# Two-layer transformer kernel: layer 1's scores in two stretches, divisions queued ahead of rotary sums, and inputs transposed by VectorE in 32x32 squares that change places by way of memory

## The chip, the cores and the metric

The kernel runs on one core of a Trainium2 chip, as one program. The metric is the time of an execution on the device in microseconds (us); lower is better. Before the change the median of three runs is 939.76 us (939.63 to 940.93). The profile is of one further execution. Engines are named as in the profile: PE is TensorE (PEld its weight loads), DVE VectorE, ACT ScalarE, POOL GpSimd, SP the engine that issues most DMAs.

## What is computed

Input x is 8 batches of 512 tokens by 256 channels, float32. Two layers follow each other; each normalises its input and adds an attention part and a feed-forward part to x.

```python
# layer 1 (names L0_*)
xn = layernorm(x)
q, k, v = xn @ Wq + bq, xn @ Wk + bk, xn @ Wv + bv      # 16 heads of 64
q, k = rope(q), rope(k)
attn = softmax(causal(q @ k.T / 8))                     # per head, 512 x 512
attention = (attn @ v) @ Wo + bo
x_scale = max(abs(xn)) / 127                            # over all batches
ffn = int8(xn / x_scale) @ int8_weight.T * x_scale * weight_scale + bias
x = x + attention + ffn
# layer 2 (names L1_*): a gated comparison of all tokens with all, and a
# feed-forward part of three 256 x 256 products
```

The change lies in layer 1's attention, whose steps fill most of the program, and in how layer 1 keeps its transposed normalised input.

## The kernel before

**Steps.** Layer 1 works in 16 steps, numbered `at`; a step is half of the heads (8) of one batch, so `b, g = divmod(at, 2)` gives batch and half. The order of instructions on every engine is written by hand: the loop `for at in range(1, last)` (L813) calls one helper after another, each appends its instructions to the queues of the engines that it uses, and every engine takes its queue strictly in order. Step 0 stands before the loop, the last step and layer 2 behind it.

**Projections.** `project_qk` (L387) makes q or k for four heads: TensorE multiplies the transposed input `xnT` with weights into PSUM (`pq`, L400), ScalarE copies it out with the bias (`l`, L405), and SP copies `l` to `y` with groups of 32 partitions swapped (L407). `turn_qk` (L410) is the rotary embedding: VectorE multiplies `l` with cosines into `h` and `y` with sines in place (both L417), and GpSimd adds the two (the rotary sum, L432). `project(at, which)` calls `project_qk` twice. `project_v` (L434) makes v (`pv`, L443), ScalarE copies it (L449), and it goes through memory to lie in another order (`va`, `vr`; `load_v`, L455).

**Scores.** The 512 queries of a head are 16 strips of 32; strip i needs 32(i+1) keys. Two strips fill one PSUM bank per half of the heads, eight heads lie beside each other, and `RUNS` (L34) cuts the strips into five runs: (15; 14, 0), (13, 1; 12, 2), (11, 3; 10, 4), (9, 5; 8, 6) and (7). For a run, `scores` (L469) lets TensorE multiply in tiles of 64x32 (`sc`, L480); `soften` (L487) lets VectorE add the mask and take each row's maximum (`nm`, L508) and ScalarE the exponential and its sum (L512); `divide` (L518) takes the reciprocals on VectorE (L523) and multiplies the rows with them on GpSimd (L531), or with `on_act` on ScalarE (L529) for the run's second pair of strips; `turn` (L539) transposes them in 32x32 squares on VectorE (L551). `weigh` (L560) multiplies all of a step's rows with v (`av`, L568), `keep_weighed` (L576) copies the result out on ScalarE, and `output_product` (L356) and `add_output` (L368) multiply with Wo (`pw`, L362) and add on VectorE (L371).

**Order of a step.** scores run 0 of this step; weigh of the step before; scores run 1; q projection of the next step; scores run 2; v projection of the next step; in even steps the transposes of the next batch's input; scores runs 3 and 4; output product of the step before; k projection of the step after next. Each run is softened, divided and turned close behind its scores.

**PSUM.** All results of TensorE go to tiles of one pool with 8 buffers, one for each of the eight banks of 512 float32 a partition (`bank`, L60). A tile takes over a bank that an earlier tile has left; its first matmul waits until the readers of that earlier tile are done.

**Input.** `look_at` (L291) takes a batch's statistics on VectorE, `prepare` (L305) normalises it (L171) and takes its greatest magnitude (L301). `transpose_x` (L312) transposes it on TensorE (8 transposes of 128x128, `pxt`, L318), ScalarE copies the two results into `xnT` (L321), and `keep_input` (L309) stores it in memory (`xnf`). Later, `fetch_input` (L183) brings it back, `round_input` (L187) scales and rounds it on GpSimd, and `clip` (L192) limits it on VectorE for the int8 product (`add_quantised`, L199). Batches 0 and 1 are fetched and clipped in steps 12 and 13, the others in the tail and layer 2.

Of the kernel before, what the change touches and what calls it, by code (L numbers as in the profile page):

```python
# [8 lines left out]
F32 = mybir.dt.float32  # L9
# [7 lines left out]
P = 128  # L17
# [27 lines left out]
def two_layers(  # L45
# [25 lines left out]
        return xpool.tile([P, NT, D], F32, tag="x1", name=name, bufs=3)  # L71

    x1_far = [far.tile([P, NT * D], F32, name=f"x1f_{b}") for b in range(B - 1)]
    xn_far = [far.tile([P, NK * S], F32, name=f"xnf_{b}") for b in range(B)]

    def load_x(b, parts=1):
        t = xpool.tile([P, NT, D], F32, tag="x", name=f"x_{b}")
# [103 lines left out]
        nc.sync.dma_start(dst.rearrange("p t n -> p (t n)"), x1_far[b])  # L181

    def fetch_input(b, r):  # L183
        nc.sync.dma_start(r.rearrange("p a n -> p (a n)"), xn_far[b])
        return r

    def round_input(r):  # L187

        r = r.rearrange("p a n -> p (a n)")
        nc.gpsimd.tensor_scalar(r, r, xs[:, 1:2], ROUND, ALU.mult, ALU.add)  # L190

    def clip(r, xq):  # L192

        r = r.rearrange("p a n -> p (a n)")
        xq_ = xq.rearrange("p k n -> p (k n)")
        nc.vector.tensor_scalar(xq_, r, -ROUND, -128.0, ALU.add, ALU.max)
        nc.vector.tensor_scalar(xq_, xq_, 127.0, 127.0, ALU.min, ALU.min)

    def add_quantised(b, half, xq, u):  # L199
        rows = slice(2 * half, 2 * half + 2)  # L200
        acc = bank(f"acc_{b}_{half}").rearrange("p (j n) -> p j n", j=2)
        for j in range(2):
            tok = bass.ts(2 * half + j, P)
            for k in range(NK):
                nc.tensor.matmul(  # L205
                    acc[:, j, :], xq[:, k, tok], w8b[:, k, :], start=(k == 0), stop=(k == NK - 1)
                )
        u = u.rearrange("p (j n) -> p j n", j=2)
        for j in range(2):
            nc.vector.scalar_tensor_tensor(  # L210
                u[:, j, :], acc[:, j, :], xs[:, 0:1], rw[:, 0, :], ALU.mult, ALU.mult
            )
        nc.gpsimd.tensor_tensor(x1s[b][:, rows, :], x1s[b][:, rows, :], u, ALU.add)
# [41 lines left out]
    with ExitStack() as c0:  # L255
# [49 lines left out]
        def prepare(b):  # L305
            norm_input(b)
            greatest_of(b)

        def keep_input(b):  # L309
            nc.sync.dma_start(xn_far[b], xnT[b].rearrange("p k n -> p (k n)"))  # L310

        def transpose_x(b):  # L312
            xn = normed.pop(b)
            xnT[b] = whole(f"xnT_{b}")
            for k in range(NK):
                pb = bank(f"pxt_{b}_{k}")
                for t in range(NT):
                    nc.tensor.transpose(  # L318
                        pb[:, bass.ts(t, P)], xn[:, t, bass.ts(k, P)], ident
                    )  # L320
                nc.scalar.copy(xnT[b][:, k, :], pb)  # L321
            if b > 0:
                keep_input(b)

# [62 lines left out]
        def project_qk(at, which):  # L387


            b, g = divmod(at, NG)  # L390
            w = wqkv[which]

            l, y = (
                prob.tile([P, 2, S], F32, tag="p", name=f"{tag}_{at}_{which}") if at == 1 else
                work.tile([P, 2, S], F32, tag=tag, name=f"{tag}_{at}_{which}", bufs=2) for tag in "ly"
            )
            for t in range(2):
                pb = bank(f"pq_{at}_{which}_{t}")
                for k in range(NK):
                    nc.tensor.matmul(  # L400
                        pb, w[:, g, k, bass.ts(t, P)], xnT[b][:, k, :],
                        start=(k == 0), stop=(k == NK - 1),
                    )
                bias = BIAS + which * NP + 2 * g + t
                nc.scalar.activation(l[:, t, :], pb, AF.Identity, bias=cs[:, bias : bias + 1])  # L405
            for n in range(4):
                nc.sync.dma_start(y[bass.ts(n ^ 1, Q)], l[bass.ts(n, Q)])  # L407
            evicted[at, which] = l, y
# [25 lines left out]
        def project_v(at, halves=(0, 1)):  # L434
# [3 lines left out]
            for half in halves:  # L438
                v = work.tile([P, 4, 2, P], F32, tag="v", name=f"v_{at}_{half}", bufs=2)
                for j in range(2):  # L440
                    pb = bank(f"pv_{at}_{half}_{j}")
                    for k in range(NK):
                        nc.tensor.matmul(  # L443
                            pb.rearrange("p (g n) -> p g n", g=2),
                            xnT[b][:, k, bass.ts(2 * half + j, P)],
                            wqkv[2][:, 2 * g : 2 * g + 2, k, :],
                            start=(k == 0), stop=(k == NK - 1),
                        )
# [87 lines left out]
        def pitch(c):  # L536
            return NT * 4 - 4 * c - 1

        def turn(at, run):  # L539

            if at not in turned:
                turned[at] = [
                    prob.tile([P, 2, 4 * pitch(c) + 1, Q], F32, tag=f"t{c}", name=f"t_{at}_{c}", bufs=1)
                    for c in range(NT)
                ]
            for i in (i for us in RUNS[run] for i in us):
                p = chances.pop((at, i))
                for c in range(i // 4 + 1):
                    n = min(4, i + 1 - 4 * c)
# [10 lines left out]
        def weigh(at):  # L560
            t = turned.pop(at)
            banks = [bank(f"av_{at}_{j}") for j in range(4)]
            for i in by_turns:
                c, m = divmod(i, 4)
                for j in range(4):
                    rows = slice(j * Q, j * Q + Q)
                    for e in range(2):
                        nc.tensor.matmul(  # L568
                            banks[j][e * L : e * L + L, i * Q :],
                            vs[at][rows, m, c, bass.ts(e, L)],  # L570
                            t[c][rows, e, m * pitch(c) + m : m * pitch(c) + NT * 4 - 4 * c, :],
                            start=(i == by_turns[0]), stop=(i == by_turns[-1]),
                        )
# [25 lines left out]
        def fetch_late(b):  # L599
# [1 line left out]
                tag, k = {2: ("vr", 0), 3: ("vr", 1), 4: ("t1", 0), 5: ("t1", 1), 6: ("t2", 0)}[b]  # L601
                fetch_output(b, by_tokens(cuts[tag][k]))
            if b > 2:
                late[b] = fetch_input(b, cuts["wo"][b % 2].rearrange("p (k n) -> p k n", k=NK))

        def round_late(b):
            round_input(late[b])

        def clip_late(b):
            xq = work.tile([P, NK, S], BF16, tag="xq", name=f"xq_{b}")  # L610
            clip(late.pop(b), xq)
            return xq

# [196 lines left out]
        x_next.append(load_x(2))  # L810
        turn(0, 3)
        project(2, 1)
        for at in range(1, last):  # L813
            b, g = divmod(at, NH)
            two = at + 2 <= last
            if g == 0 and b < B - 1:
                fetch(b)
            scores(at, 0)
            turn(at - 1, 4)
            soften(at, 0)  # L820
            if at == last - 3:
                scale_of_x()
            weigh(at - 1)
            keep_weighed(at - 1)
            if at == 1:
                load_rest()
                load_second()
                fetch(0)
            turn_qk(2 * at + 2, 1)
            load_v(at)  # L830
            if at in (last - 3, last - 2):
                s_ = at - last + 3
                fetch_output(s_, output_tile(f"x1e_{s_}"))
                xnl = fetch_input(s_, work.tile([P, NK, S], F32, tag="xnl", name=f"xnl_{s_}"))
            divide(at, 0)
            turn_qk(2 * at + 3, 1)
            if at == last - 2:
                first_norm = norm(0, xpool.tile([P, NT, D], F32, tag="x", name="yn_0"))
            scores(at, 1)
            soften(at, 1)  # L840
            turn(at, 0)
            if at == 2:
                look_at(2)
            elif at == 4:
                spread_rest()
                spread_second()
            elif g == 1 and 1 <= b < B - 2:
                look_at(b + 2)
            divide(at, 1)
            if at == last - 1:  # L850
                first_norm()
            project(at + 1, 0)
            if at in (last - 3, last - 2):
                round_input(xnl)
            scores(at, 2)
            soften(at, 2)
            turn_qk(2 * at + 2, 0)
            turn(at, 1)
            if at in (last - 3, last - 2):
                xq = work.tile([P, NK, S], BF16, tag="xq", name=f"xq_{s_}")  # L860
                clip(xnl, xq)
            divide(at, 2)
            if at == 2:
                prepare(2)
            elif g == 1 and 1 <= b < B - 2:
                prepare(b + 2)
            if at == last - 1:
                turn_qk(2 * at + 3, 0)
            if at == 1:
                nc.gpsimd.tensor_tensor(bob, bob, rw[:, 2, :], ALU.add)  # L870
                add_biases(0)
            project_v(at + 1)
            if at == last - 1:
                break
            if g == 0 and b < B - 1:
                transpose_x(b + 1)
                if b + 2 < B:
                    x_next.append(load_x(b + 2))
            scores(at, 3)
            soften(at, 3)  # L880
            turn_qk(2 * at + 3, 0)
            turn(at, 2)
            divide(at, 3)
            scores(at, 4)
            soften(at, 4)
            if at in (last - 3, last - 2):
                for half in range(2):
                    add_quantised(s_, half, xq, line(f"u_{s_}_{half}"))
            finish(at - 1)
            turn(at, 3)  # L890
            if two:
                project(at + 2, 1)
            divide(at, 4)
            if g == 0 and b < B - 1:
                add_biases(b)
            if at == last - 4:
                greatest()


        at = last  # L900
        scores(at - 1, 3)
        soften(at - 1, 3)
        nc.sync.dma_start(w2, second.rearrange("j (k p) n -> p j k n", p=P))
        turn(at - 1, 2)
        divide(at - 1, 3)
        scores(at - 1, 4)
# [21 lines left out]
        divide(at, 1)  # L928
        keep_weighed(at - 1)
        load_v(at)  # L930
        late[2] = fetch_input(2, work.tile([P, NK, S], F32, tag="xnl", name="xnl_2"))
        add_biases(B - 1)
        turn(at, 0)
        scores(at, 2)
# [143 lines left out]
```

## Time and profile before

| what | value |
|---|---|
| time, median of 3 runs | 939.76 us (939.63 to 940.93) |
| the profiled execution: its time | 939.1 us |
| the profiled execution: its span, first to last instruction | 937.2 us |
| granted TensorE clock, mean | 0.999 of full |
| 600 to 700 us: busy PE, DVE, ACT, POOL | 98.79, 91.29, 59.59, 74.45 us |
| 700 to 937.2 us: the same | 233.49, 182.11, 118.84, 89.96 us |
| rows of L417, y and h: mean | 1729 ns, 1243 ns, 64 each |
| row of L432: mean | 2596 ns, 62 |
| row of L551 (all shapes): mean | 366 ns, 640 |

A row of the profile has the line of the kernel, the engine, the operation, output<-inputs by tile names, partitions x elements, and a count; times are busy time and the mean of one. A timeline has the start and length of each instruction, or of several alike that follow each other; an idle time ahead of it stands in brackets with what ended it. The chain follows the last instruction back, step by step, to what released it. The span is the time between first and last instruction; the execution's own time is somewhat longer.

### The profile page before, as it was taken

To read this page: it belongs to the slowest core of one execution; us is meant where nothing else is said; L and a number is where in the kernel's file an instruction comes from. 1 tells how busy PE (TensorE), PEld (TensorE's weight loads), DVE (VectorE), ACT (ScalarE), POOL (GpSimd) and SP (SyncE) were. 2 spreads that over 40 slices of the span, in tenths; PEclk is the share of its full clock that TensorE was granted. 3 is DMA by queue.
4 is the path that set the end of the run, shared out by engine and by line. 5 is a ranking of instruction groups with operands and counts; after the bars stand their busy time and mean duration, and the time that the engine had idled before them with its cause. 6 is when DMAs were issued, how large, how long until landed. Compare 5 with 4: busy or idle time off the path is not lost.

```text
span 937.2 us, 27414 instructions
## 1 busy us (share of the span) xinstructions
PE 923.8 (99%) x10491; PEld 600.8 (64%) x10491; DVE 787.4 (84%) x2431; ACT 533.0 (57%) x1488; POOL 540.0 (58%) x688
## 2 busy tenths in 40 slices
PE   9998999999999999999999999999999999999998
PEld 5446565656666575757565656666657777777776
DVE  4998889898799889978997899899899588888854
ACT  3585555656575656474747566555667434445553
POOL 2676765655665757566665756678666424444311
PEclk9999999999999999999999999999999999999999
DMA  7667453525443545263535435453444132211011
GB/s 212 193 166 201 112 128 126 122 80 138 146 105 96 133 136 131 75 159 92 136 91 160 108 98 137 136 145 106 103 114 126 47 101 79 76 57 39 23 34 34
DMA packets 60930, 105.40 MB, mean 112 GB/s; under 512 B 7552, under 2 KB 38272, under 8 KB 60800
## 3 DMA queue, kind: packets, MB, share of 16 engines
q1 hardware_dynamic: 58928, 102.01, 40.1%
q10 hardware_dynamic: 1872, 1.64, 0.7%
q8 instruction: 83, 1.36, 0.6%
q14 instruction: 47, 0.39, 0.1%
HBM read 39.14 MB, written 28.84 MB: 73 GB/s over the span
## 4 chain that ended last, share of the span: by engine, by line
PE 92%; DVE 4%; issue 1%; ACT 1%; POOL 1%; SPq 0%; DMA 0%; DVEq 0%; ACTq 0%; POOLq 0%
PE pq L400 22%; PE av L568 14%; PE sc L480 13%; PE pw L362 12%; PE pv L443 10%; PE po L727 5%; PE pg L689 3%; PE pvv L701 3%; PE pk L674 3%; PE trc L714 1%; PE plr L240 1%; PE c L646 1%; DVE t L551 1%; PE acc L205 1%; DVE p L508 1%
## 5 line engine op out<-in xcount | busy, mean ns | idle before, releaser
L512 ACT ACTIVATE p<-p,nm 128x64 f32<-128x64 f32 (+15 forms) x512 | 259.9, 512 | 123.1 <-DVE nm L508 98.3
L531 POOL TENSOR_SCALAR p<-p,rs 128x512 f32<-128x512 f32 (+4 forms) x504 | 263.3, 543 | 44.0 <-DVE rs L523 41.9
L432 POOL TENSOR_TENSOR h<-h,y 128x1024 f32<-128x1024 f32 x62 | 161.0, 2596 | 188.9 <-DVE y L417 106.6
L508 DVE CUSTOM_DVE_ANT_0 p<-sc,cmask 128x64 f32<-128x64 f32 (+15 forms) x512 | 190.3, 434 | 61.5 <-PE sc L480 61.5
L551 DVE STREAM_TRANSPOSE t<-p 128x256 f32<-128x256 f32 (+3 forms) x640 | 192.1, 366 | 18.2 <-POOL p L531 18.1
L480 PE MATMUL sc<-h,h 64*32 64x416 f32 (+15 forms) x4096 | 138.7, 393 | 1.9 <-POOL h L432 1.2
L568 PE MATMUL av<-t,vr 32*64 32x192 f32 (+15 forms) x4096 | 128.8, 392 | 4.0 <-issue 4.0
L568 PEld LDWEIGHTS av<-t,vr 32*64 32x64 f32 x4096 | 123.2, 131 | 9.1 <-issue 7.8
L480 PEld LDWEIGHTS sc<-h,h 64*32 64x32 f32 x4096 | 78.8, 106 | 76.0 <-issue 56.5
L405 ACT ACTIVATE l<-pq,cs 128x512 f32<-128x512 f32 x128 | 84.7, 683 | 66.8 <-PE pq L400 54.4
L417 DVE TENSOR_TENSOR y<-y,cs 128x1024 f32<-128x1024 f32 x64 | 110.7, 1729 | 5.8 <-DMA y<-l 5.3
L362 PE MATMUL pw<-wo,att 128*128 128x256 f32 x512 | 114.8, 382 | 0.0
L400 PE MATMUL pq<-xnT,wq 128*128 128x512 f32 x256 | 114.6, 599 | 0.2 <-ACT xnT L321 0.2
L443 PE MATMUL pv<-wv,xnT 128*128 128x512 f32 x256 | 114.3, 599 | 0.0
L400 PE MATMUL pq<-xnT,wk 128*128 128x512 f32 x256 | 112.9, 593 | 0.6 <-DVE nm L508 0.6
L362 PEld LDWEIGHTS pw<-wo,att 128*128 128x128 f32 x512 | 95.9, 190 | 18.5 <-issue 6.1
L512 ACT ACTIVATION_READ_ACCUMULATOR p<-p,nm 128x1 f32 x512 | 97.3, 190 | 0.0
L400 PEld LDWEIGHTS pq<-xnT,wk 128*128 128x128 f32 x256 | 48.6, 190 | 56.6 <-issue 54.1
L443 PEld LDWEIGHTS pv<-wv,xnT 128*128 128x128 f32 x256 | 47.3, 190 | 57.9 <-issue 54.1
L417 DVE TENSOR_TENSOR h<-l,cs 128x1024 f32<-128x1024 f32 x64 | 79.5, 1243 | 4.5 <-ACT l L405 4.5
L400 PEld LDWEIGHTS pq<-xnT,wq 128*128 128x128 f32 x256 | 47.2, 190 | 56.0 <-issue 48.8
L582 ACT ACTIVATE att<-av,cs 128x512 f32<-128x512 f32 x64 | 38.7, 688 | 71.4 <-PE av L568 71.4
(113 smaller groups left out, 949.8 us busy)
## 6 DMA issues: line engine op xcount, KB each, us to landing
y<-l SPq DMA_DIRECT2D x256, 128.0 KB, 2.3
va<-v SPq DMA_DIRECT2D x32, 512.0 KB, 3.1
vr<-va SPq DMA_DIRECT2D x64, 256.0 KB, 4.8
x<-in_x SPq DMA_DIRECT2D x15, 512.0 KB, 4.2
xnf<-xnT SPq DMA_DIRECT2D x8, 512.0 KB, 3.3
x1f<-x SPq DMA_DIRECT2D x7, 512.0 KB, 2.7
out<-y SPq DMA_DIRECT2D x14, 256.0 KB, 2.2
cut_wo<-xnf SPq DMA_DIRECT2D x5, 512.0 KB, 4.2
```

Of the source, the lines that this page charges most:

```text
L362: nc.tensor.matmul(pw[:, j, :], atts[at, p][:, tok], wo[:, 4 * (at % NH) + p, :], start=(p == 0), stop=(p == 3),)
L400: nc.tensor.matmul(pb, w[:, g, k, bass.ts(t, P)], xnT[b][:, k, :], start=(k == 0), stop=(k == NK - 1),)
L405: nc.scalar.activation(l[:, t, :], pb, AF.Identity, bias=cs[:, bias : bias + 1])
L417: nc.vector.tensor_tensor(dst, src, table[:, None, :].to_broadcast([P, 2, S]), ALU.mult)
L432: (engine or nc.gpsimd).tensor_tensor(h, h, y, ALU.add)
L443: nc.tensor.matmul(pb.rearrange("p (g n) -> p g n", g=2), xnT[b][:, k, bass.ts(2 * half + j, P)], wqkv[2][:, 2 * g : 2 * g + 2, k, :], sta ...
L480: nc.tensor.matmul(scored[at, i][e][j * Q : j * Q + Q, :], q[rows, j % 2, bass.ts(i, Q)], k[rows, j % 2, :n], start=True, stop=True,)
L508: nc.vector.tensor_tensor_reduce(p[:, e, col : col + n], sc, cmask[:, S - n :], -1.0 / L**0.5, BIG, ALU.add, ALU.min, nm[:, c : c + 1],)
L512: nc.scalar.activation(p[:, e, col : col + n], p[:, e, col : col + n], AF.Exp, bias=nm[:, c : c + 1], scale=-1.0, accum_out=sm[:, c : c + 1],)
L531: nc.gpsimd.tensor_scalar(p, p, rs[:, c : c + 1], 1.0, ALU.mult, ALU.mult)
L551: nc.vector.transpose(turned[at][c][:, :, at_ : at_ + (n - 1) * pitch(c) + 1 : pitch(c), :], p[:, :, c * P : c * P + n * Q].rearrange("p e ...
L568: nc.tensor.matmul(banks[j][e * L : e * L + L, i * Q :], vs[at][rows, m, c, bass.ts(e, L)], t[c][rows, e, m * pitch(c) + m : m * pitch(c) ...
```

## The change

Steps 0 and 1 and layer 2 keep their order. In steps 2 to 14:

- **Scores in two stretches.** TensorE's order becomes: weigh of the step before; scores runs 0 and 1; q projection; the first half of the v projection; scores runs 2, 3 and 4; the second half of v; output product; k projection. (Step 14 ends behind the whole v projection; runs 2 and 3 follow behind the loop.)
- **Divisions ahead of sums.** Run 0's divisions are queued on GpSimd ahead of the rotary sum of the second four heads, run 1's ahead of that of the next step's q. Runs 0 and 1 are softened, then come a pair of rotary products, run 0's transposes, another pair of products, run 1's transposes, and run 2 is softened behind all of that. One of the four rotary embeddings of a step moves to the start of the next step. The second strips of run 3 are divided on ScalarE.
- **Normalising.** `look_at` and most of `prepare` move to the start of a step.
- **Inputs.** For batches 2 to 7, `turn_x` replaces the transposes on TensorE and the copies on ScalarE: VectorE transposes 32x32 squares (two instructions of 128x512), SP writes the result to `xnf` and reads it back with the squares in their places, in four transfers. `xnT` therefore holds the tokens in another order, and the projections and the clip read it in pieces of 32 elements; `weigh` reads v's blocks with two indices exchanged. Batches 0 and 1 still go through TensorE and are stored in four transfers; every later fetch is four transfers.

The diff, cut to its core (line numbers of the parts left out are not shown):

```diff
     def fetch_input(b, r):
-        nc.sync.dma_start(r.rearrange("p a n -> p (a n)"), xn_far[b])
+        r_ = r.rearrange("p (a n) -> p a n", a=4)
+        for m in range(4):
+            nc.sync.dma_start(r_[bass.ts(m, Q)], xn_far[b][:, m].rearrange("(a k) n -> k a n", a=4))
...
+        def turn_x(b):
+            xn = normed.pop(b)
+            t = work.tile([P, 4, NK, NT, Q], F32, tag="xnl", name=f"xs_{b}")
+            for k in range(NK):
+                nc.vector.transpose(
+                    t[:, :, k].rearrange("p m t r -> p t m r"),
+                    xn[:, :, bass.ts(k, P)].rearrange("p t (m q) -> p t m q", m=4),
+                )
+            nc.sync.dma_start(
+                xn_far[b], t.rearrange("p m k t r -> p m (k t r)")
+            )
+            fetch_input(b, turned_input(b))
...
                     nc.tensor.matmul(
-                        pb, w[:, g, k, bass.ts(t, P)], xnT[b][:, k, :],
+                        pb.rearrange("p (t a r) -> p t a r", a=4, r=Q), w[:, g, k, bass.ts(t, P)],
+                        xnT[b][:, k].rearrange("p a (t r) -> p t a r", r=Q),
...
-        for at in range(1, last):
+        for at in range(2, last):
...
-            scores(at, 0)
-            turn(at - 1, 4)
-            soften(at, 0)
             if at == last - 3:
                 scale_of_x()
             weigh(at - 1)
+            if at > 2:
+                turn_qk(2 * at + 1, 0)
+            if at == 2 or g == 1 and 1 <= b < B - 2:
+                look_at(b + 1 + g)
+            turn_qk(2 * at + 2, 1)
+            if g == 0 and 1 < b < B - 2:
+                prepare(b + 1)
             keep_weighed(at - 1)
...
+            scores(at, 0)
+            scores(at, 1)
+            soften(at, 0)
+            project_qk(2 * at + 2, 0)
+            soften(at, 1)
             divide(at, 0)
             turn_qk(2 * at + 3, 1)
...
+            project_qk(2 * at + 3, 0)
...
             turn(at, 0)
             divide(at, 1)
-            project(at + 1, 0)
-            scores(at, 2)
-            soften(at, 2)
             turn_qk(2 * at + 2, 0)
             turn(at, 1)
-            divide(at, 2)
...
             if g == 0 and b < B - 1:
-                transpose_x(b + 1)
+                turn_x(b + 1)
...
-            project_v(at + 1)
-            scores(at, 3)
-            soften(at, 3)
-            turn_qk(2 * at + 3, 0)
-            turn(at, 2)
-            divide(at, 3)
-            scores(at, 4)
-            soften(at, 4)
+            project_v(at + 1, (0,))
+            for run in (2, 3, 4):
+                scores(at, run)
+            soften(at, 2)
+            soften(at, 3)
+            project_v(at + 1, (1,))
+            divide(at, 2)
+            turn(at, 2, slice(0, 1))
+            divide(at, 3, on_act=True)
+            turn(at, 2, slice(1, 2))
+            soften(at, 4)
...
-            finish(at - 1)
-            turn(at, 3)
+            for half in range(2):
+                output_product(at - 1, half)
+            turn(at, 3, slice(0, 1))
+            divide(at, 4)
+            turn(at, 3, slice(1, 2))
+            for half in range(2):
+                add_output(at - 1, half)
+            turn(at, 4)
             if two:
                 project(at + 2, 1)
-            divide(at, 4)
```

## The prediction

> **What bounds the kernel now.** I read the page's busy times first, then the waits of the matmul engine, the chain in order of time over one step of the loop, and the timelines of VectorE and GpSimd over the same step. Page and waits:
>
> ```profile
> PE 923.8 (99%) x10491; PEld 600.8 (64%) x10491; DVE 787.4 (84%) x2431; ACT 533.0 (57%) x1488; POOL 540.0 (58%) x688
> ...
> PE av L568 <- issue: 4.0, 4, 2.3
> ```
>
> TensorE never starves: its longest wait for anything is 2.3 us. Only what TensorE does, or a new wait of it, can move the end. One step (chain in order of time; start, length, what):
>
> ```profile
> 344.12 1.89 PE sc L480 x45
> 346.01 7.96 PE av L568 x165
> 353.97 2.05 PE sc L480 x57
> 356.01 7.06 PE pq L400 x16
> 363.08 1.94 PE sc L480 x64
> 365.02 7.06 PE pv L443 x16
> 372.08 2.32 PE sc L480 x80
> 374.40 7.10 PE pw L362 x32
> 381.51 6.87 PE pq L400 x16
> ```
>
> A step is 44.25 us, 45.1 where it also has the transposes of line 318 (0.88 us, seen at 326.96 in the same chain). Here pq is 6.87 behind pw but 7.06 behind scores: leaving a stretch of scores costs 0.19. A projection pass of 512 columns is 6.87/16 = 0.43; a run of scores is two bank widths in two passes, 1.72, so the run of 1.94 has 0.22 of entry. VectorE in this step (start, length):
>
> ```profile
> 347.84 1.22 DVE L417 TENSOR_TENSOR h<-l,cs 128x1024 f32<-128x1024 f32 x1
> 348.97 1.22 DVE L417 TENSOR_TENSOR y<-y,cs 128x1024 f32<-128x1024 f32 x1
> 350.11 0.23 DVE L523 RECIPROCAL rs<-sm 128x2 f32<-128x2 f32 x2
> 350.26 1.19 DVE L417 TENSOR_TENSOR h<-l,cs 128x1024 f32<-128x1024 f32 x1
> 351.37 3.38 DVE L417 TENSOR_TENSOR y<-y,cs 128x1024 f32<-128x1024 f32 x1
> ...
> 364.19 0.56 DVE L508 CUSTOM_DVE_ANT_0 p<-sc,cmask 128x384 f32<-128x384 f32 x1 [1.63 <-PE sc L480]
> ```
>
> and GpSimd:
>
> ```profile
> 350.32 3.34 POOL L432 TENSOR_TENSOR h<-h,y 128x1024 f32<-128x1024 f32 x1 [5.00 <-DVE rs L523]
> 353.64 4.14 POOL L531 TENSOR_SCALAR p<-p,rs 128x512 f32<-128x512 f32 x6
> 357.75 2.37 POOL L432 TENSOR_TENSOR h<-h,y 128x1024 f32<-128x1024 f32 x1
> 363.51 3.64 POOL L531 TENSOR_SCALAR p<-p,rs 128x448 f32<-128x448 f32 x8
> ```
>
> The reader is to see two things. VectorE waits for scores (1.63 us at 364.19), so it stands ahead of TensorE at run 2. And rotary products and GpSimd exclude each other: a product alone takes 1.14 (347.84 to 348.97); the sum issued at 350.32 takes 3.34 instead of 2.37 because it stands behind the product of 350.26, the product issued at 351.37 takes 3.38 because it stands behind that sum, and the first division of 353.64 stands behind that product. Their times add up.
>
> **What TensorE gains.** Steps 2 to 14 have one stretch of scores less between projections (0.22 + 0.19) and run 0 no longer stands alone ahead of av (1.89 - 1.72 = 0.17): about 0.6 a step, 13 steps, 7.8 us. Six batches lose their transposes on TensorE: 6 x 0.88 = 5.3. If nothing else took their place: 13.1 us.
>
> **What takes their place.** I walk one new step, 0 being av's start. TensorE unhindered: av to 8.0, runs 0 and 1 to 11.7, q projections (7.06) to 18.8, half of v (3.43) to 22.2, runs 2 and 3 (0.22 + 3.44) to 25.9, run 4, second half of v at 26.5, pw, pq, end 43.65. But PSUM has eight banks, and runs 2 to 4 write ten. By the built order run 4 takes the two banks of strips 11 and 3, and v's second half those of strips 10 and 4; both are free only when VectorE has done the maxima (L508) of run 2. TensorE's order is fixed: v, pw and pq stand behind that wait.
>
> VectorE reaches run 2 so: maxima of run 0 start 1.2 after their scores (345.23 against 344.05), at 9.2, and take 2.61 (to 347.84 in the trace); run 1 2.76: 14.6; reciprocals 14.75. Then the change has in this order: two products, run 0's transposes (2.71), reciprocals, two products, run 1's transposes (2.76), then run 2. Alone that is 2.27 + 2.71 + 0.15 + 2.27 + 2.76, ending at 24.9. But GpSimd's queue is now: run 0's divisions, a rotary sum, run 1's divisions; run 0's transposes wait for the first, run 1's for the last. With the exclusion everything from 14.75 is one file: four products 4 x 1.14, divisions 3.0 (4.14 less the 1.1 behind the product), sum 2.3, divisions 3.64, together 13.5: 28.2, and after the last division a last transpose: 28.4. In the old step the same work lay beside av and the q projection, and VectorE still waited for scores.
>
> From 28.4, strips 11 and 3 are read after 1.25 and strips 10 and 4 after 2.6 (the sequence behind 364.19), so v's second half starts at 31.1 instead of 26.5: TensorE waits 4.6. Then v 3.5, pw 6.85, pq 6.87: 48.3. Against 44.25 that is +4.05. In steps with an even number VectorE also turns the inputs just ahead of run 2's maxima: two transposes of 512 columns, for which there is no row; between twice the pitch of a 256-column one (2 x 0.65) and twice its full 0.408 (2 x 0.82), I take 1.4, nearer the pitch since they follow each other. End 49.7 against 45.1: +4.6. Six pairs of steps: 6 x 8.65 = 52 us.
>
> Some steps have more VectorE work ahead of run 2's maxima, free before and on the path now: normalising and maximum of batch 2 (4 x 0.53 + 1.2, partly beside divisions, +1.4) and of batch 7 (with a sum in its way, +4); the spreads of step 4 (+1); rounding (1.12) and clip (0.67 + 0.88) of steps 12 and 13, the clip behind a sum (+4 each): 14.5. Step 14 has first_norm and two more products ahead: TensorE would be done with run 3 at 29.4 and gets its bank at about 36; the chain of before already leaves TensorE there (679 to 696 is VectorE and GpSimd), so no slack takes it up: +6.
>
> **The rest.** ScalarE loses twelve copies (0.59 each) and gains four divisions a step (2.0 us): it idles 18 us a step, and they stand between exponentials that VectorE awaits later: 0; without that cover 2 a step. GpSimd loses those (1.9) outside the file above: 0. SP's queue carries the turned inputs: one write (3.3 to landing by the row xnf) and four reads (4.2 by cut_wo), 29.8 to 37.5, and pq needs them at 42.9: hidden, 5 us to spare; v's stores stand behind, wanted only by the next step's loads. Keeps and late fetches become four transfers instead of one, far ahead of use: 0. The q and k projections read their inputs in 16 pieces of 32: no row; 0 if a piece costs nothing (v's two pieces cost nothing: 7.06 as well), at most what a break costs in line 318's short passes (0.88/8 - 0.43/4, some 3 ns), 16 x 3 ns x 16 passes behind the wait, 0.8 a step, 10 us. I take 0. Clip in pieces: 0 to 0.33 (0.667 against the slower row 0.994) eight times; 0.
>
> **Rules against rows.** The Trainium skill, "VectorE: DVE Perf Modes", Summary, sends 128x128 transposes to TensorE and only 32x32 ones to VectorE. By the rows the move takes 0.88 from TensorE and puts 1.4 on VectorE. By busy shares (99% against 84%) the rule would be wrong here; at this place of the step VectorE ends last, so the rule is right: +0.5 net a batch. "TensorE: Matmul & The Clock Gate", Part 1, halves the clock after an idle window of about 3.4 us until a busy one has passed. No wait of this trace is that long and its clock row is full, so the row says no cost. My waits are 3.8 and 5.2 us at a stretch: by the rule an even step could lose 1.7 to 3.4 more, an estimate of 10 to 20 us for six. I keep it out of the sum and in the upper end.
>
> **Sum.** 937.2 + 52 + 14.5 + 6 = 1009.7, plus the 1.9 by which the profiled execution (939.1) exceeds its span: 1011.6. I say 1010. The median before, 939.76, is 0.7 above that execution; nothing is corrected for it.
>
> **Rivals.**
> - The exclusion costs little, because GpSimd's work slips between products. Then run 2's maxima start at 24.9 and v at 27.5: end 44.75 and 46.1, +0.5 and +1.0, 9 us in six pairs, 10 for the extra work and step 14: 958. For it: the products lie next to transposes, which run freely beside GpSimd. Against: products and sums cover each other fully at 350.
> - The clock gate answers the new waits: 1010 + 10 to 20 and the pieces' 10, about 1035. For it: the length of the waits. Against: nothing shows it.
> - Faster: TensorE never waits, 939.1 - 13.1 = 926. It needs run 2's maxima to start by 23.9 (26.5 less 2.6), 14.7 after run 0's; the work between is 15.7 even without exclusion, so VectorE would have to do it faster than every row. For it: VectorE is busy only 84%.
> - The change doesn't do what it says: in the built order it does.
>
> **Numbers.** First case 0.66 (995 to 1030), exclusion hidden 0.20 (950 to 995), clock gate 0.08, faster 0.06. 0.2%, some 2 us, is about what this measurement can tell from no change; a tie needs gain and wait to cancel: 0.02, taken from the second and fourth. Range 955 to 1030.
>
> **What would show it.** Right: TensorE's busy share falls to about 92%; its waits name VectorE's maxima (nm) ahead of sc run 4 and pv, 4 to 6 us a step; L417 and L432 grow longer; steps of 48 to 50 us. Wrong: steps of 44 to 45 with waits under 1 us (second case), no waits at all (926), or a clock row below nine.

## The result and the profile after

The changed kernel takes 1036.21 us (median of 4 runs, 1032.65 to 1038.82), the kernel before 940.35 beside it (4 runs, 939.63 to 941.96): ratio 1.1018, interval 1.0997 to 1.1039. It is slower, as forecast, but 26 us above the forecast and 6 above the range. The profiled execution takes 1034.79 us, 95.7 more than the one of before, with a span of 1033.0 and a mean granted clock of 0.949.

The page of the changed kernel: busy times, then TensorE and its granted clock in 40 slices.

```profile
PE 946.4 (92%) x10443; PEld 603.2 (58%) x10443; DVE 815.6 (79%) x2443; ACT 542.2 (52%) x1524; POOL 545.7 (53%) x640
## 2 busy tenths in 40 slices
PE   8999979897989798989898969699797999999998
...
PEclk9999989898989898989898989889898999999999
```

TensorE is at 92%, as the prediction said. But its busy time went up by 22.6 us although it has 48 instructions fewer, and the clock row is an 8 in about every second slice. Before, it was all nines:

```profile
PEclk9999999999999999999999999999999999999999
```

The waits of TensorE (engine, tile, line, what it waited for: us in all, times, longest):

```profile
PE sc L515 <- DVE nm L543: 73.7, 13, 10.7
PE av L603 <- issue: 4.8, 3, 2.3
```

One wait in each of 13 steps, for VectorE's maxima. The timeline of TensorE in a step with an odd number (start, length, what, idle before):

```profile
377.25 7.87 PE L603 MATMUL av<-t,vr 32*64 32x512 f32 x256
385.05 3.98 PE L515 MATMUL sc<-h,h 64*32 64x512 f32 x112
388.96 7.13 PE L434 MATMUL pq<-xnT,wq 128*128 128x512 f32 x16
395.93 3.60 PE L478 MATMUL pv<-wv,xnT 128*128 128x512 f32 x8
399.46 3.74 PE L515 MATMUL sc<-h,h 64*32 64x384 f32 x128
407.18 1.31 PE L515 MATMUL sc<-h,h 64*32 64x256 f32 x16 [3.99 <-DVE nm L543]
408.52 5.64 PE L478 MATMUL pv<-wv,xnT 128*128 128x512 f32 x8
414.00 7.07 PE L396 MATMUL pw<-wo,att 128*128 128x256 f32 x32
```

Run 4 waits 3.99 us for its bank. Then the second half of v takes 5.64; the first half, eight matmuls of the same shape, took 3.60 at 395.93. The windows of the same stretch say why (last columns: granted clock, DMA share, GB/s):

```profile
404.00:405.00 1.00, 0.00 (x0) 0.00 (x0) 0.73 (x3) 0.00 (x0) 1.00 (x4) 1.00 0.95 251
405.00:406.00 1.00, 0.00 (x0) 0.00 (x0) 1.00 (x5) 0.00 (x0) 1.00 (x2) 0.83 1.05 361
406.00:407.00 1.00, 0.00 (x0) 0.00 (x0) 1.00 (x7) 0.56 (x2) 1.00 (x1) 0.50 0.12 39
...
411.00:412.00 1.00, 1.00 (x2) 0.34 (x1) 0.53 (x6) 1.00 (x6) 0.43 (x1) 0.50 0.02 8
412.00:413.00 1.00, 1.00 (x3) 0.53 (x2) 0.25 (x1) 1.00 (x6) 1.00 (x3) 0.75 0.00 0
413.00:414.00 1.00, 1.00 (x4) 0.38 (x2) 1.00 (x4) 1.00 (x5) 1.00 (x4) 1.00 0.00 0
```

The clock falls to half during the wait, at about 405.7, and comes back at about 412.5: some 6.8 us, of which TensorE works 5.3. Over the whole trace there are 14 such stretches, 105.8 us together, in which TensorE is busy 65.7: at half speed that loses 32.8 us.

What VectorE and GpSimd do meanwhile (timelines; of the maxima only the first of runs 0 and 2):

```profile
386.23 0.69 DVE L543 CUSTOM_DVE_ANT_0 p<-sc,cmask 128x512 f32<-128x512 f32 x1 [6.03 <-PE sc L515]
...
391.74 1.19 DVE L452 TENSOR_TENSOR h<-l,cs 128x1024 f32<-128x1024 f32 x1
392.85 1.22 DVE L452 TENSOR_TENSOR y<-y,cs 128x1024 f32<-128x1024 f32 x1
395.25 2.79 DVE L586 STREAM_TRANSPOSE t<-p 128x256 f32<-128x256 f32 x9 [1.18 <-POOL p L566]
397.97 0.20 DVE L558 RECIPROCAL rs<-sm 128x4 f32<-128x4 f32 x2
398.08 2.35 DVE L452 TENSOR_TENSOR h<-l,cs 128x1024 f32<-128x1024 f32 x1
...
405.81 0.52 DVE L543 CUSTOM_DVE_ANT_0 p<-sc,cmask 128x384 f32<-128x384 f32 x1
```

```profile
391.85 5.18 POOL L566 TENSOR_SCALAR p<-p,rs 128x512 f32<-128x512 f32 x6 [9.16 <-DVE rs L558]
396.99 2.37 POOL L467 TENSOR_TENSOR h<-h,y 128x1024 f32<-128x1024 f32 x1
399.32 5.69 POOL L566 TENSOR_SCALAR p<-p,rs 128x448 f32<-128x448 f32 x8
404.97 2.36 POOL L467 TENSOR_TENSOR h<-h,y 128x1024 f32<-128x1024 f32 x1
```

VectorE now idles 6.03 us under av, because no scores of this step lie ahead of it; from 391.74 on, the file forecast runs as written: products, divisions stretched by products (5.18 against 4.14 before), a product stretched by the sum (2.35), transposes that wait for divisions. Run 2's maxima start at 405.81, 28.6 after av.

The 95.7 us split so: TensorE idles 86.6 us of its span against 13.4 (+73.2); the half clock costs 32.8; the remaining -10.3 I put down to TensorE work that the change takes away. Some 5 us could stand under either of the first two: in all thirteen steps a stretch of scores behind the wait is drawn out by 0.44 (run 4 takes 1.31 instead of 0.87 at full clock), but v behind it would have waited for its own bank meanwhile.

### The profile page after: what moved, and what is told of

The parts are those of the page before. It is cut to its first block, busy times and chain, and to the rows that moved or that the text cites. A ratio compares the mean times of both kernels' runs of the same rounds, so it can differ in the third digit from the quotient of the medians.

```text
span 1033.0 us, 27338 instructions
## 1 busy us (share of the span) xinstructions
PE 946.4 (92%) x10443; PEld 603.2 (58%) x10443; DVE 815.6 (79%) x2443; ACT 542.2 (52%) x1524; POOL 545.7 (53%) x640
## 4 chain that ended last, share of the span: by engine, by line
PE 66%; DVE 14%; POOL 10%; issue 4%; DMA 3%; ACT 1%; SPq 1%; DVEq 0%; POOLq 0%; ACTq 0%
PE av L603 13%; PE pq L434 12%; PE pw L396 10%; POOL p L566 8%; PE pv L478 8%; DVE p L543 6%; PE po L762 5%; PE sc L515 5%; PE pk L709 3%; PE pg L724 3%; PE pvv L736 3%; DVE t L586 3%; DMA vr<-va 2%; PE c L681 1%; DVE y L452 1%
## 5 line engine op out<-in xcount | busy, mean ns | idle before, releaser
L566 POOL TENSOR_SCALAR p<-p,rs 128x512 f32<-128x512 f32 (+6 forms) x456 | 273.6, 623 | 211.4 <-DVE rs L558 208.6
L515 PE MATMUL sc<-h,h 64*32 64x64 f32 (+15 forms) x4096 | 144.8, 405 | 73.9 <-DVE nm L543 73.7
L467 POOL TENSOR_TENSOR h<-h,y 128x1024 f32<-128x1024 f32 x62 | 149.2, 2407 | 118.8 <-DVE y L452 108.2
L515 PEld LDWEIGHTS sc<-h,h 64*32 64x32 f32 x4096 | 87.1, 108 | 130.0 <-issue 114.9
L478 PE MATMUL pv<-wv,xnT 128*128 128x512 f32 x256 | 136.7, 686 | 0.4
L603 PE MATMUL av<-t,vr 32*64 32x384 f32 (+15 forms) x4096 | 129.6, 397 | 5.8 <-issue 4.8
L603 PEld LDWEIGHTS av<-t,vr 32*64 32x64 f32 x4096 | 113.1, 132 | 30.9 <-issue 24.2
L452 DVE TENSOR_TENSOR h<-l,cs 128x1024 f32<-128x1024 f32 x64 | 104.1, 1627 | 7.9 <-ACT l L440 7.9
L452 DVE TENSOR_TENSOR y<-y,cs 128x1024 f32<-128x1024 f32 x64 | 84.8, 1325 | 23.0 <-DMA y<-l 23.0
L478 PEld LDWEIGHTS pv<-wv,xnT 128*128 128x128 f32 x256 | 55.6, 224 | 78.3 <-issue 67.5
```

The source lines that it names most:

```text
L452: nc.vector.tensor_tensor(dst, src, table[:, None, :].to_broadcast([P, 2, S]), ALU.mult)
L467: (engine or nc.gpsimd).tensor_tensor(h, h, y, ALU.add)
L478: nc.tensor.matmul(pb.rearrange("p (g n) -> p g n", g=2), xnT[b][:, k, 2 * half + j], wqkv[2][:, 2 * g : 2 * g + 2, k, :], start=(k == 0), ...
L515: nc.tensor.matmul(scored[at, i][e][j * Q : j * Q + Q, :], q[rows, j % 2, bass.ts(i, Q)], k[rows, j % 2, :n], start=True, stop=True,)
L566: nc.gpsimd.tensor_scalar(p, p, rs[:, c : c + 1], 1.0, ALU.mult, ALU.mult)
L603: nc.tensor.matmul(banks[j][e * L : e * L + L, i * Q :], vs[at][rows, c, m, bass.ts(e, L)], t[c][rows, e, m * pitch(c) + m : m * pitch(c) ...
```

## The experiments

My theory: run 2's maxima come late by the one file of products, sums and divisions; with ten banks wanted of eight, TensorE waits for them, and the clock's answer to that wait is the part I left out. The rivals: the exclusion matters little, or the input path (squares, memory, pieces) costs.

**The inputs alone.** The order of before, with `turn_x`, pieces of 32 and transfers in four:

```diff
             if g == 0 and b < B - 1:
-                transpose_x(b + 1)
+                turn_x(b + 1)
```

> The kernel before with the change's new input path alone (squares on VectorE, pieces of 32, four transfers); the order of the steps is that of before. My theory (the waits come from the order, the path itself is cheap): TensorE loses 6 x 0.88 us of transposes and waits for nothing new, so 934 to 937 us. Rival (reading the inputs in 16 pieces slows the projections, up to some 0.8 to 1.5 us a step): no gain or 950 to 960, with pq and pv passes longer than 0.43 us.

Measured 940.54, ratio 1.0022 (1.0013 to 1.0031): neither the gain that my theory forecast nor a cost of pieces. The rows of the projections read 599 ns (q) and 600 (k) a matmul, against 599 and 593 before. Nearly all of k's 7 ns come from one projection, which takes 8.5 us at half clock behind a wait; the others behind the output product take 6.96 to 7.04, against 6.96 before. So pieces cost nothing worth the name. What eats the gain is the trip through memory, which the k projection awaits in this order (chain in order of time, start, length):

```profile
329.75 1.20 DVE xs L325 x2
...
330.97 4.09 DMA xnf<-xs
...
336.40 3.10 DMA xnT<-xnf
339.50 0.14 issue
339.63 5.39 PE pq L434 x12
```

From squares to projection 9.9 us, waited for 4 times, 6.6 us in all. In the change itself no such wait exists: the step is longer there.

**The order alone.** The change with the old transposes:

```diff
-                turn_x(b + 1)
+                transpose_x(b + 1)
```

> The change with the inputs of batches 2 to 7 still transposed on TensorE: the new order alone. Theory: nearly the whole loss is there; 1.4 us of VectorE work leave the path of even steps and 0.88 come back on TensorE, ahead of run 2's scores where TensorE waits anyway, so 3 to 8 us less than the change, 1026 to 1033, with waits for the maxima of 60 to 70 us and the clock still halved in nearly every step. Rival (the round trip of the inputs makes the loss): near 940.

Measured 1028.77, ratio 1.0959 (1.0932 to 1.0987). Waits for maxima 60.6 us instead of 73.7. The order is nearly the whole loss; the new input path costs 7.4 us there. In the change the two squares of an even step lie on the path just ahead of run 2's maxima (chain in order of time):

```profile
354.59 1.26 DVE xs L325 x2
355.85 0.44 DVE p L543
```

**The wait filled.** The change with five useless matmuls of 512 columns, ahead of the scores of strips 8 and 6 into their bank, so that TensorE is busy while it would have waited:

```diff
+                if fill is not None and us is RUNS[run][-1]:
+                    for _ in range(FILL):
+                        nc.tensor.matmul(
+                            banks[0].rearrange("p (a r) -> p a r", a=4), ident, fill[:, 0],
...
+            scores(at, 3, fill=xnT[(at + 1) // NH])
```

> The change with five useless matmuls of 512 columns, ten passes or 4.3 us, put between runs 2 and 4 into the bank of strips 8 and 6, which is written over by its scores: TensorE works through most of its wait. If the halved clock costs what the longer pv passes say (some 24 us), the clock stays full and the time falls although work is added: 1005 to 1018. If pv is long for another reason (banks, pieces), the time stays at 1036 or grows.

Measured 1019.37, ratio 1.0862 (1.0841 to 1.0882): 17 us faster than the change (1 us short of what I forecast), with some 52 us of useless work more (12 steps of about 4.4). TensorE's timeline, the next half of v behind the filling (L510):

```profile
394.36 4.56 PE L510 MATMUL sc<-xnT,ident 128*128 128x512 f32 x10
398.85 1.53 PE L522 MATMUL sc<-h,h 64*32 64x288 f32 x48
400.58 3.67 PE L479 MATMUL pv<-wv,xnT 128*128 128x512 f32 x8 [0.21 <-PE sc L522]
```

That half is back at 3.67 and the clock at full in this step. The mean clock is 0.987; the half clock costs 11.7 us instead of 32.8, of which 8.3 lie in steps 11 to 14, whose waits the filling does not cover. Less waiting cannot be the reason: TensorE's idle time fell from 86.6 to 35.8 us, no more than the filling took. So the clock term is shown, and is worth at least 17 us.

**Run 2 earlier.** The change with the first half of v and run 2 (scores and maxima) ahead of run 1's transposes:

```diff
             turn_qk(2 * at + 2, 0)
+            if at < last - 1:
+                project_v(at + 1, (0,))
+                scores(at, 2)
+                soften(at, 2)
             turn(at, 1)
```

> The change with the maxima of run 2 put ahead of run 1's transposes on VectorE (half of the v projection and run 2's scores are issued ahead of that, TensorE's order stays). Theory (the wait is the place of run 2's maxima on VectorE): strips 11 and 3 are read when TensorE wants the banks, the waits fall to 0.5 to 3 us a step, the clock stays full, 955 to 975. Rival (VectorE simply has too much work for the shorter steps): the wait moves to run 3's maxima at its old size, over 1010.

Measured 969.66, ratio 1.0333 (1.0312 to 1.0354): 67 us of the 96 come back by the place of one run's maxima. The transposes that wait for the last divisions no longer stand ahead of them; run 4 does not wait in the ordinary steps, and the second half of v waits 0.5. The waits for maxima that are left come to 32.5 us; the output product has the most of them (13.6 us in 12 waits).

**Sums ahead of divisions.** The change with GpSimd's order of before in the two places:

```diff
-            divide(at, 0)
             turn_qk(2 * at + 3, 1)
+            divide(at, 0)
...
-            divide(at, 1)
             turn_qk(2 * at + 2, 0)
+            divide(at, 1)
```

> The change with the divisions of runs 0 and 1 put back behind the two rotary embeddings that they were moved ahead of. Theory (VectorE's products, GpSimd's sums and divisions add up, and run 1's transposes wait for the divisions): another sum of 2.3 us and a product pair lie ahead of the divisions, run 2's maxima start some 3 us later a step, 1060 to 1090. Rival (putting divisions first is what delays the sums and costs the time): faster than the change, under 1025.

Measured 1076.12, ratio 1.1454 (1.1425 to 1.1483), waits for maxima 115.0. So the divisions ahead of sums, taken alone, help this order by 40 us.

**One sum behind.** The sum that stands between run 0's and run 1's divisions moved behind the latter:

```diff
-            turn_qk(2 * at + 3, 1)
+            turn_products(2 * at + 3, 1)
...
             divide(at, 1)
+            turn_sum(2 * at + 3, 1)
```

> The change with the rotary sum between the divisions of run 0 and those of run 1 moved behind the latter on GpSimd; the products stay where they are. Theory: the sum leaves the file, but run 1's divisions then wait for run 0's transposes, so run 2's maxima start 1.0 to 1.8 us earlier a step and fewer waits are long enough for the clock to fall: 995 to 1020. Rival (GpSimd's place doesn't matter, VectorE's order alone sets the wait): 1030 to 1040.

Measured 1028.7, ratio 1.0942 (1.0920 to 1.0965): a miss. The ordinary waits did fall by 1.2 us as I expected (4.0 to 2.8 in odd steps, 5.2 to 4.0 in even ones), but those of steps 11, 12 and 14 grew (7.8 to 8.9, 10.7 to 13.1, 4.5 to 7.8) and that of step 13 stayed. And a wait of 2.8 us still costs clock, as this step shows:

```profile
400.97 1.31 PE L525 MATMUL sc<-h,h 64*32 64x256 f32 x16 [2.81 <-DVE nm L553]
402.31 4.62 PE L488 MATMUL pv<-wv,xnT 128*128 128x512 f32 x8
```

Half of v takes 4.62 instead of 3.6, the clock standing at half for 3.4 us.

**The exclusion taken away.** In two of a step's four embeddings, squares of the same tiles in place of the products, which this kernel leaves out:

```diff
-            turn_qk(2 * at + 3, 1)
+            turn_qk_free(2 * at + 3, 1)
...
-            turn_qk(2 * at + 2, 0)
+            turn_qk_free(2 * at + 2, 0)
```

> The change with the products of two of the four rotary embeddings of a step (those that lie between run 0's maxima and run 2's) replaced by 32x32 transposes of the same tiles: as many VectorE instructions, 1.3 us instead of 1.14 each, but with one input. The rotary products of these two are left out of what is computed. If products and GpSimd's work exclude each other, the file falls apart and run 2's maxima start at about 25.6 instead of 28.4 in the step: waits of 1.5 to 3 us, clock mostly full, 965 to 995. If VectorE's own order is what takes the time: 1036 to 1045.

Measured 984.93, ratio 1.0497 (1.0477 to 1.0517). The squares take as long as a free product (1.21), yet the divisions beside them run at their own pace. GpSimd's timeline of the step that answers to the one above:

```profile
371.50 3.17 POOL L577 TENSOR_SCALAR p<-p,rs 128x512 f32<-128x512 f32 x6 [9.16 <-DVE rs L569]
374.62 2.36 POOL L465 TENSOR_TENSOR h<-h,y 128x1024 f32<-128x1024 f32 x1
376.96 3.63 POOL L577 TENSOR_SCALAR p<-p,rs 128x448 f32<-128x448 f32 x8
```

5.18 became 3.17 and 5.69 became 3.63: 4 us, what the exclusion adds to the divisions in each step. Run 2's maxima start 25.2 us behind av instead of 28.6. Run 4's ordinary waits fall to 0.6 us in odd steps and 1.8 to 2.1 in even ones, and the clock stays full there. The exclusion is shown, and with the clock it is worth 51 us.

**The inputs earlier.** The order of before, the squares and their write (in steps 4, 6, 8 and 10) behind run 1's divisions, the reads where they were:

```diff
             divide(at, 1)
+            if g == 0 and 2 < at < last - 3:
+                turn_x(b + 1)
...
-                turn_x(b + 1)
+                if at in (2, last - 3):
+                    turn_x(b + 1)
+                fetch_input(b + 1, turned_input(b + 1))
```

> The order of before with the new input path, and in steps 4, 6, 8 and 10 VectorE's two squares and the write to memory some 8 us earlier, ahead of run 2's maxima, the reads at their old place. If the path alone stood at 940.5 only because the k projection waited for the round trip (6.6 us of waits), those waits go and TensorE keeps the 5.3 us of transposes: 933 to 936, below both kernels. If pieces or the longer VectorE queue cost it, it stays at 940.

Measured 937.05 (12 runs, 935.15 to 938.08), ratio 0.9966 (0.9956 to 0.9976): some 3 us (0.3%) less than the kernel before, which took 938.62 to 941.96 in 16 runs beside it, and so faster than both kernels, though 1 us short of what I forecast. One wait for the memory is left (2.2 us), and behind it the clock halves once, for 3.4 us. With the trip hidden, moving the transposes off TensorE pays, though less than the 5.3 us of their busy time.

**Run 0 behind weigh, alone.** The same kernel, with run 0's scores and maxima behind weigh, beside run 1:

```diff
-            scores(at, 0)
+            if at == 1:
+                scores(at, 0)
...
+            if at > 1:
+                scores(at, 0)
+                scores(at, 1)
+                soften(at, 0)
```

> The order of before with the early inputs (937), and from step 2 on the scores of run 0 behind weigh, next to run 1, and their maxima there; runs 2, 3 and 4 stay where before had them. TensorE saves some 0.2 us a step by it (2 to 3 us in all). Theory: the old place let VectorE take run 0's maxima, products and divisions under the 8 us of av; now VectorE idles there and is late with everything behind, so the weigh of the next step waits for transposes: 955 to 985. Rival (only runs 2 to 4 in one stretch and their ten banks are to blame): 933 to 938.

Measured 1005.96, ratio 1.0717 (1.0697 to 1.0737): 69 us for moving one run, more than I expected. By the traces 52 of them are idle time of TensorE and 14 the half clock behind it. TensorE's largest waits name no maxima of scores here, so it is not the banks. VectorE gets nothing to do under av (first fence, its maxima of run 0 with the idle time ahead of them), and is late for the transposes of the next weigh (second fence, TensorE):

```profile
377.55 0.69 DVE L542 CUSTOM_DVE_ANT_0 p<-sc,cmask 128x512 f32<-128x512 f32 x1 [5.47 <-PE sc L514]
```

```profile
368.58 7.86 PE L602 MATMUL av<-t,vr 32*64 32x512 f32 x256 [2.48 <-DVE t L585]
...
418.08 2.88 PE L602 MATMUL av<-t,vr 32*64 32x512 f32 x25 [4.69 <-issue]
```

For the second of these waits the profile names nothing; VectorE's last transposes of that step start at 417.54, half a microsecond ahead of av.

**Run 0 ahead again, in the change.** Run 0 and the fourth embedding back at their old places, the squares behind run 0's transposes:

```diff
+            scores(at, 0)
+            soften(at, 0)
...
-            if at > 2:
-                turn_qk(2 * at + 1, 0)
...
-            scores(at, 0)
+            divide(at, 0)
+            turn_qk(2 * at + 3, 1)
             scores(at, 1)
-            soften(at, 0)
...
+            early = g == 0 and not clips and at < last - 1
+            if early:
+                turn_x(b + 1)
```

> The change with run 0's scores and maxima back ahead of weigh (three stretches of scores instead of two), the fourth rotary embedding back behind run 3's maxima, and the squares of the inputs behind run 0's transposes; runs 2 to 4 still stand in one stretch, divisions stay ahead of sums. Theory: run 2's maxima then start when their scores are done, TensorE waits at most 1 us a step, the clock stays full, and one stretch less (0.4 a step) and no transposes on TensorE remain as gain: 926 to 938. Rival (ten banks for runs 2 to 4 are too many whatever stands ahead): over 960.

Measured 986.3, ratio 1.0503 (1.0485 to 1.0522): 50 us better than the change, but a miss. An ordinary odd step is down to 45.5 us; its waits are small but not gone:

```profile
385.07 0.87 PE L515 MATMUL sc<-h,h 64*32 64x256 f32 x16 [0.63 <-DVE nm L543]
386.41 3.67 PE L478 MATMUL pv<-wv,xnT 128*128 128x512 f32 x8 [0.47 <-DVE nm L543]
```

Where VectorE has more than the ordinary to do, TensorE still pays: of 36.9 us in the 13 waits ahead of run 4, 26.7 lie in steps 2 and 11 to 14. The half clock still costs 12.1 us. VectorE waits 1.79 for exponentials that stand behind the copies of the q projection on ScalarE; that order was not tried the other way round. So these moves together give back about half of the loss, and the rival's number, over 960, came: with ten banks in one stretch VectorE has no slack. How much each of the three moves gives was not taken apart.

## Why the prediction failed where it did

- **What bounds, and the new wait: right.** TensorE at 92%, one wait a step for VectorE's maxima ahead of run 4, behind it the second half of v.
- **The walk: right to 0.3 us.** In the odd step above, run 2's maxima start 28.6 us after av (28.4 forecast), run 4 29.9 (29.65), the second half of v 31.3 (31.1). The exclusion behind it is shown by the kernel with squares for products. The rival in which the exclusion costs little (958) falls.
- **The step that failed: the clock, a term put at nothing.** "The clock gate answers the new waits" got a chance of 0.08, and "I keep it out of the sum and in the upper end". It answered all thirteen new waits of the loop: 32.8 us by the trace (1.7 of them in step 1, ahead of these waits), or 28 if run 4's 5 are counted as wait. The page that I weighed, the Trainium skill's "TensorE: Matmul & The Clock Gate", Part 1, speaks of an idle window of about 3.4 us. I compared my waits of 3.8 and 5.2 with the full clock row of a kernel whose longest wait was 2.3, which said nothing of longer ones. The traces agree with the length of that window and not with its being wholly idle: about 2 us of waiting in such a window sufficed (last section).
- **The rival's number was luck.** Its "about 1035" came out, yet not by its sum: it holds 10 us for pieces that cost nothing, and counted the clock in six even steps only.
- **The waits: 85.6 forecast (72.5 net and 13.1 of gain), 73.2 measured.** Of the 12 too many, ordinary steps have 9: 64.5 was forecast for six pairs, and six pairs of the measured 4.0 and 5.2 are 55.2. Some 5 of the 9 are the second short wait, of v, which shows as the stretched run 4. The extra work of steps 2 to 14 has most of the rest.
- **TensorE's gain: 13.1 forecast, 10.3 left** in the remainder of the split.
- **The sum.** 1011.6 + 32.8 - 12.4 + 2.8 = 1034.8, the profiled execution. The waits, taken 12.4 too long, hid part of the clock's 32.8; the gain, taken 2.8 too large, went the other way. That the forecast missed this execution by some 25 us and not by 34 is luck.
- **Costed at nothing, rightly:** the pieces of 32, and the memory trip in this order (in the order of before it is not hidden).
- **The squares** are on the path: a pair takes 1.26 us in the chain instead of the 1.4 forecast, and keeping the new input path off this order is worth 7.4 us for six batches. The rule for transposes that the prediction weighed from the Trainium skill's "VectorE: DVE Perf Modes" stands there under "Rules for kernel authors". It comes out right in this order, by these 7.4 us, and wrong in the order of before with early squares, where the move gained some 3.
- Not separated: how much of the last steps' waits is each of rounding, clip and normalising.

## What to carry to other kernels

Count the banks that a stretch of matmuls writes; if they are more than the pool has, find the instruction that frees the last one and walk to it along its own engine's queue, with every operation that excludes another added in a file. Before moving work to the other side of a long matmul stretch, ask what the other engine did beneath that stretch: run 0's maxima beneath av were worth 69 us where they were moved away alone, against 13 that TensorE was to save by the whole change. Price a new wait of TensorE with the clock's answer: in the traces of this case none under 1.99 us was answered and every one of 3.14 us or more was, and the work behind it ran at half speed, in most cases for 3.4 or 6.8 us.

## What was not expected of the hardware

How long a wait is does not alone decide whether the clock halves. In the twelve traces all waits of 3.14 us and more were answered and none under 1.99, but between these both occur. In the changed kernel one of 2.13 us at 116.3 was answered and one of 2.32 at 70.5 was not; with the inputs earlier, one of 2.17 at 156.1 was; with the order alone, one of 3.09 at 554.0 was not.

What decides is how the wait falls on a fixed beat. The drops of one trace lie whole multiples of 3.41 us apart (in the changed kernel at 200.86, 252.06 and 303.26, that is 51.2 or 15 x 3.41), and the half clock lasts 3.41 us or a multiple of it. I cut the changed kernel's trace at these times: in each interval of 3.41 us ahead of a drop TensorE idles at least 2.02 us, and in no other interval at full clock more than 1.63. Over all twelve traces the border lies near 2 us: the least idle time ahead of a drop is 1.74, the most without one 2.00.

Useless matmuls in the place of a wait made the kernel 17 us faster. A square transpose of VectorE (1.21 us for 128x1024) runs beside GpSimd's divisions without a trace of exclusion; a product of the same length adds about 1 us to the divisions that it meets.
